# Four chained layers on one Trainium2 core: padded scan sums, layer 3's own image pool, and the next pair's first step made in layer 3

## The chip, the cores and the metric

The kernel runs on one core of a Trainium2 chip. A core has five engines, each with its own instruction queue that is worked off in order: TensorE (PE in the profile, with PEld for its weight loads), VectorE (DVE), ScalarE (ACT), GpSimd (POOL) and SyncE (SP), which here only issues DMAs. The engines share an on-chip memory of 128 partitions; TensorE writes its sums to a second one, PSUM. The metric is the time of one execution on the device in microseconds, as the median of several.

## The reference

The input x is 16 images of 192 channels and 64 x 64 points, in float32. Four layers follow one another, and each adds its result to x. Ahead of each layer x is group-normalised (32 groups of 6 channels).

```
x = x + L0(_gn(x))     # a small network on each point of each channel (tanh, sigmoid)
x = x + L1(_gn(x))     # x and its four shifts by one point, times a 192 x 960 matrix
x = x + L2(_gn(x))     # four state-space scans over the image
x = x + L3(_gn(x))     # depthwise 3x3, 5x5, 1x7, 7x1, then a 192 x 192 matrix, batch norm, clip(0, 6)
```

Layer 2 runs each image through four scans (k = 0 row by row, 1 column by column, 2 and 3 the same backwards) with N = 16 states per channel:

```
dA = jnp.exp(d[..., None] * A)                          # d = delta = softplus(dts + bias)
h = dA * h + (d * u)[..., None] * Bt[:, :, None, :]
y = jnp.einsum('bkdn,bkn->bkd', h, Ct)
...
ys = jnp.moveaxis(ys, 0, -1) + xs * Ds.reshape(K, D)[None, :, :, None]
```

and adds the four results up in image order. Layer 3's batch norm takes its mean and variance over all 16 images, so that its last step can only come at the very end.

## The kernel before

**Tiling.** Two images make a pair: 384 rows of 4096 points, in three tiles (j = 0, 1, 2; NT = 3) of 128 partitions. There are 8 pairs. For each, `front` (L372) does layers 0 and 1 and the projections of layer 2, `scans` (L782) does layer 2, and `layer3` (L1053) does layer 3 up to z, its result ahead of the batch norm. The front of the next pair runs beside the scans of this one: `scans` drives it as a generator, a few instructions per step. Pair 0's front runs alone at the start, and after pair 7 a last stage (L1174 on) computes the batch norm, clips and adds.

**Scans.** For each tile j, direction k (in ORDER = 1, 3, 0, 2) and chunk m of 1024 points there is one entry t of `todo`, 48 per pair, and for each t there are 16 steps, one per state n. Each step s = 16 t + n is a product on DVE (`product`, L910: the spread row of B times du = delta * u), a scan on DVE (`scan`, L913), a copy of the last state on ACT, and a product with C on POOL. Beside them `load_c` fetches the row of C (SP), `decay` makes dA three steps ahead (ACT), and `spread` (L897) brings a row of B into PSUM with two matmuls, two steps ahead. Its PSUM tile is one of two, so it waits for the scan two steps before. `add_up` (L931) sums the products over the states in PSUM on PE, LATE = 4 steps behind, and after the last state ACT copies the sum to X (row-wise directions) or Xt (column-wise).

**The step of a chunk.** delta and du of chunk t + 1 are made during chunk t by `step_rest` (L867): at n = 4 its four matmul instructions write v, ACT applies softplus, and at n = 8 POOL makes du. v and the sum ysum share one PSUM tile: v waits until ACT has copied the sum of the chunk before out (at n = 3), and the next sum's first state (at n = 5) waits until softplus has read v. At n = 4 the loop issues, in this order, the product, the scan, `decay(s + 3)`, `spread(s + 2)`, and then `step_rest`. The load of the rows for chunk t + 2 (`load_dt`, at n = 4, SP) shares one buffer with that of t + 1, so it waits for v.

**The end of a tile.** `finish` (L963) adds Xt to X in four pieces, each followed by two bn_stats for the group norm of layer 3, and stores X to `x3_d`. For tiles 0 and 1 this lies in the next tile's first chunk; for tile 2 (adds on DVE) it comes after the last step.

**Order.** Everything in `scans` is kept in program order on its engine (`_Engines(tc, True)`). Everything in `layer3` is ordered at compile time by a scheduler with program order as its priority. Memory is given out pool by pool, in the order in which the pools are opened; pools that are opened after others were closed lie where those were, and their first use waits for the last use of what lay there.

**Layer 3.** It loads the three tiles of x3 into the middle of a padded tile xp of 70 x 70 points (L1064), zeroes the edges and builds diagonal matrices of the taps' weights on POOL (L1070 to L1077), does the group norm, normalises (L1085), and then goes over four row blocks c and three tiles j. Of the 29 taps of a group (c, j), GP_TAPS = 8 are products on ACT added up by POOL (L1106), PE_TAPS = 7 are matmuls with the diagonals (L1111), which also add POOL's sum g (L1123), and the other 14 are multiply-adds on DVE into the same PSUM tile (L1129; the last one writes y). There are two such PSUM tiles. Then PE multiplies the three y with the 192 x 192 matrix (L1143), ACT copies z out, DVE takes its statistics, and z is stored. The first pieces of the next pair's scans (its load of xn, dt and bp, the normalising, v, delta, du, at L984 to L990) follow after that.

**Last stage.** For each of the 24 tiles z and x3 are loaded, ACT applies scale, shift and relu, DVE clips and adds, and the sum is stored (L1221 to L1231).

Of the kernel before, what the change touches and what calls it, by code (L numbers as in the profile page):

```python
# [22 lines left out]
P = 128  # L23
C = 192
NT = 3
# [24 lines left out]
PE_TAPS = 7  # L50
GP_TAPS = 8

# [52 lines left out]
def conv_preact_kernel(ctx: ExitStack, tc: tile.TileContext, a: dict):  # L105
# [10 lines left out]
    x3_d = dram.tile([npair, NT * P, L], F32, name="x3_d")  # L116
# [3 lines left out]
    wt_d = dram.tile([GR, NG, 2 * P], F32, name="wt_d")  # L120

# [79 lines left out]
    with tc.tile_pool(name="prep", bufs=1) as prep, tc.tile_pool(  # L201
# [83 lines left out]
        for part, w in (  # L285
            (wc[:, :, 2:5, 2:5], w3x3),
            (wc[:, :, 3, :], w1x7),
            (wc[:, :, :, 3], w7x1),
        ):
            nc.vector.tensor_tensor(part, part, w, ALU.add)  # L290

# [18 lines left out]
    sets = [Made(n) for n in range(2)]  # L310

# [25 lines left out]
    def group_norm(E, st, stat, ps, gm, rstd):  # L337

        mv = stat.tile([P, NT, 2], F32, name="mv", tag="mv")
        mean = stat.tile([P, NT], F32, name="mean", tag="mean")  # L340
        d2 = stat.tile([P, NT], F32, name="d2", tag="d2")
        half = stat.tile([P, NT], F32, name="half", tag="half")
        E.dve.memset(half, -0.5)
        for j in range(NT):
            E.dve.bn_aggr(mv[:, j, :], st[:, j, :, :].rearrange("p c s -> p (c s)"))
        E.dve.tensor_copy(mean, mv[:, :, 0])

        def mean_of(src):
            s = ps("gn_sum")
            for jo in range(NT):  # L350
                for n, (b, ji) in enumerate(INTO[jo]):
                    E.pe.matmul(
                        s[:, jo : jo + 1],
                        grp[:, b, :],
                        src[:, ji : ji + 1],
                        start=(n == 0),
                        stop=(n == len(INTO[jo]) - 1),
                    )
                yield
            return s[:, :NT]  # L360

        s = yield from mean_of(mean)
        E.dve.tensor_scalar(gm, s, 1.0 / 6.0, None, ALU.mult)
        E.dve.tensor_tensor(d2, mean, gm, ALU.subtract)
        E.dve.tensor_tensor(d2, d2, d2, ALU.mult)
        E.dve.tensor_tensor(d2, d2, mv[:, :, 1], ALU.add)
        s = yield from mean_of(d2)
        E.dve.tensor_scalar(d2, s, 1.0 / 6.0, 1e-5, ALU.mult, ALU.add)
        E.gps.tensor_tensor(rstd, d2, half, ALU.pow)
# [412 lines left out]
    def scans(i, o, st3, nxt):  # L782

        E = _Engines(tc, True)
        with ExitStack() as es:
# [5 lines left out]
            two = pool("l2two", 2)  # L791
# [8 lines left out]
            X = one.tile([P, L], F32, name="X")  # L800
# [18 lines left out]
            def load_bp(t):  # L819
                if t < T:  # L820
                    j, k, at, first = todo[t]
                    bps[t] = two.tile([BP, LC], BF16, name="bp")
                    E.sp.dma_start(out=bps[t], in_=o.bp[k, :, at : at + LC])

            def load_dt(t):
                if t < T:
                    j, k, at, first = todo[t]
                    dts[t] = one.tile([32 + RD, 512], F32, name="dt")
                    src, r = (o.dtp, RD * (k // 2)) if k % 2 else (o.dt, RD * (2 + k // 2))
                    for h in range(2):  # L830
                        E.sp.dma_start(
                            out=dts[t][32 * h : 32 * h + RD, :],
                            in_=src[r : r + RD, at + 512 * h : at + 512 * h + 512],
                        )

            def load_xn(j):
                if j < NT:
                    xns[j] = one.tile([P, L], F32, name="xn")
                    E.sp.dma_start(out=xns[j], in_=row_tiles(o.x2)[:, j, :])
# [27 lines left out]
            def step_rest(t):  # L867


                j, k, at, first = todo[t]  # L870
                dt = dts.pop(t)
                v = py.tile([P, LC], F32, name="v", tag="ysum")
                for h in range(2):
                    rows = slice(32 * h, 32 * h + RD)
                    E.pe.matmul(
                        v[:, 512 * h : 512 * h + 512],
                        dtw[rows, k, j, :],
                        dt[rows, :],
                        start=True,
                        stop=True,  # L880
                    )
                delta = two.tile([P, LC], F32, name="delta")
                E.table(SOFTPLUS)
                E.act.activation(delta, v, AF.Softplus, bias=dtb[:, k, j : j + 1])
                yield
                du = two.tile([P, LC], F32, name="du")
                E.gps.tensor_tensor(image(du), image(delta), seq(xns[j], k, at, LC), ALU.mult)
                made[t] = delta, du
# [42 lines left out]
            def add_up(s):  # L931
# [8 lines left out]
                to = (Xt if k % 2 else X)[:, at : at + LC]  # L940
                if n == 1:
                    ysum[t] = py.tile([P, LC], F32, name="ysum", tag="ysum")
                    for c in range(LC // 512):
# [5 lines left out]
                        elif k != ORDER[0]:  # L949
                            E.pe.matmul(ysum[t][:, cs], ident, to[:, cs], start=True, stop=False)  # L950
# [9 lines left out]
                if n == N - 1:  # L960
                    E.act.copy(to, ysum[t])

            def finish(j):  # L963

                def add(c):
                    x = X[:, 1024 * c : 1024 * c + 1024]
                    eng = E.gps if j < NT - 1 else E.dve
                    eng.tensor_tensor(
                        image(x), image(x), columns(Xt)[:, 16 * c : 16 * c + 16, :], ALU.add
                    )  # L970

                def stats(c):
                    for h in range(2 * c, 2 * c + 2):
                        E.dve.bn_stats(st3[:, j, h, :], X[:, 512 * h : 512 * h + 512])

                for at in range(10):
                    if at in (0, 2, 4, 6):
                        add(at // 2)
                    if at in (3, 5, 7, 9):
                        E.later(lambda c=at // 2 - 1: stats(c))  # L980
                    yield
                E.sp.dma_start(out=row_tiles(x3_d[i])[:, j, :], in_=X)

            load_xn(0)  # L984
            load_dt(0)
            load_bp(0)
            norm_xn(0)
            for _ in step_rest(0):
                pass
            load_dt(1)  # L990
# [8 lines left out]
            gstep = iter(())  # L999
            for s in range(total):  # L1000
# [4 lines left out]
                if n == 2:  # L1005
                    load_bp(t + 1)
                if n == 4:
                    load_dt(t + 2)
# [4 lines left out]
                scan(s)  # L1013
                if s + 3 < total:
# [9 lines left out]


# [4 lines left out]
                elif n == 4:  # L1030
                    gstep = step_rest(t + 1) if t + 1 < T else iter(())
                    next(gstep, None)
# [18 lines left out]
            E.between()  # L1051

    def layer3(i, st3):  # L1053
        E = _Engines(tc, False)
        with tc.tile_pool(name="l3s", bufs=1) as stat, tc.tile_pool(name="l3x", bufs=1) as xk, tc.tile_pool(
            name="l3w", bufs=1
        ) as w_, tc.tile_pool(name="l3", bufs=2) as wk, tc.tile_pool(
            name="l3_pt", bufs=2, space=PSUM
        ) as pt, tc.tile_pool(name="l3_pz", bufs=4, space=PSUM) as pz:
            S = HW + 6  # L1060
            xp = xk.tile([P, NT, S, S], F32, name="xp")
            inside = slice(3, 3 + HW)
            for j in range(NT):
                nc.sync.dma_start(  # L1064
                    out=xp[:, j, inside, inside], in_=image(row_tiles(x3_d[i])[:, j, :])
                )
            pw = load("pw", [P, len(BLOCKS), P], w_)
            diag = w_.tile([P, NT, PE_TAPS, P], F32, name="diag")
            for edge in (slice(0, 3), slice(3 + HW, S)):
                nc.gpsimd.memset(xp[:, :, edge, :], 0.0)  # L1070
                for j in range(NT):
                    nc.gpsimd.memset(xp[:, j, inside, edge], 0.0)
            for j in range(NT):
                for t, (ty, tx) in enumerate(TAPS[:PE_TAPS]):
                    nc.gpsimd.tensor_scalar(
                        diag[:, j, t, :], ident, wc[:, j, ty, tx : tx + 1], None, ALU.mult
                    )  # L1077
# [5 lines left out]
            for j in range(NT):  # L1083
                v = xp[:, j, inside, inside]
                normalise(nc.vector, v, v, gm, rstd, j)  # L1085
            zst = stat.tile([P, NT, 8, 6], F32, name="zst")
            def window(j, c, rows, tap):
                return xp[:, j, c + tap[0] : c + tap[0] + rows, tap[1] : tap[1] + HW]
# [3 lines left out]

            own = PE_TAPS + GP_TAPS
            for c in range(4):
                ys = []
# [42 lines left out]
                for jo in range(NT):  # L1138
                    z = wk.tile([P, 1024], F32, name="z")
# [18 lines left out]
            nc.sync.dma_start(out=zstat_d[i], in_=zmv.rearrange("p j s -> p (j s)"))  # L1158

    def pair(i, q, more):  # L1160

        with tc.tile_pool(name="st3", bufs=1) as p3:
            st3 = p3.tile([P, NT, 8, 6], F32, name="st3")
            scans(i, sets[q], st3, None if more is None else (more, sets[1 - q]))
            layer3(i, st3)

    with tc.tile_pool(name="f_ps", bufs=1, space=PSUM) as ps:
        for _ in front(0, sets[0], _Engines(tc, False), Banks(ps, 8), True):
            pass
    for i in range(npair):  # L1170
        pair(i, i % 2, i + 1 if i + 1 < npair else None)


    with tc.tile_pool(name="fin", bufs=1) as fin, tc.tile_pool(  # L1174
# [45 lines left out]
        with tc.tile_pool(name="last", bufs=2) as lp:  # L1220
            for i in range(npair):  # L1221
                for j in range(NT):
                    z = lp.tile([P, L], F32, name="zl")
                    r = lp.tile([P, L], F32, name="rl")
                    nc.sync.dma_start(out=z, in_=row_tiles(z_d[i])[:, j, :])
                    nc.scalar.dma_start(out=r, in_=row_tiles(x3_d[i])[:, j, :])
# [3 lines left out]
                    nc.vector.scalar_tensor_tensor(r, z, 6.0, r, ALU.min, ALU.add)  # L1230
                    nc.sync.dma_start(out=row_tiles(out[i])[:, j, :], in_=r)  # L1231
# [107 lines left out]
```

## Time and profile before

| | |
|---|---|
| time, median of 3 runs (28011.66 to 28014.21) | 28012.72 us |
| profiled execution: time, and its span | 28007.89 us, 28006.0 us |
| start to the first scan of pair 0 | 1213.6 us |
| first to last scan of a pair, pairs 0 to 6 / pair 7 | 2954 to 2962 / 2784 us |
| last scan of a pair to first scan of the next | 366 us, 7 times |
| last layer-3 multiply-add of pair 7 to the end | 396.5 us |
| busy: DVE, PE, POOL, ACT | 86%, 83%, 74%, 58% |

A line of the timeline has the start and the duration in us, the engine (a name that ends in q is its queue issuing a DMA), the line of the kernel, the operation, output <- inputs, and how many such instructions were merged. In brackets is the idle time of the engine just before, and what ended it. Line L64 is a helper through which all of `scans` and `front` issues, so there the tiles tell the operations apart. A matmul of float32 is two instructions, so one group's seven diagonals in two halves are 28. A line of the waits names the engine and what it was about to do, what it waited for, the total in us, how often, and the longest.

### The profile page before, as it was taken

To read this page: it belongs to the slowest core of one execution; us is meant where nothing else is said; L and a number is where in the kernel's file an instruction comes from. 1 tells how busy PE (TensorE), PEld (TensorE's weight loads), DVE (VectorE), ACT (ScalarE), POOL (GpSimd) and SP (SyncE) were. 2 spreads that over 40 slices of the span, in tenths; PEclk is the share of its full clock that TensorE was granted. 3 is DMA by queue.
4 is the path that set the end of the run, shared out by engine and by line. 5 is a ranking of instruction groups with operands and counts; after the bars stand their busy time and mean duration, and the time that the engine had idled before them with its cause. 6 is when DMAs were issued, how large, how long until landed. Compare 5 with 4: busy or idle time off the path is not lost. (4 is left out here: it accounts for less than half of the span.)

```text
span 28006.0 us, 208082 instructions
## 1 busy us (share of the span) xinstructions
PE 23305.0 (83%) x57140; PEld 9559.7 (34%) x57140; DVE 24196.3 (86%) x15397; ACT 16122.6 (58%) x23044; POOL 20813.2 (74%) x10440
## 2 busy tenths in 40 slices
PE   8799977999689986999779997899968998676663
PEld 4343323333233332333324332333323333222221
DVE  0399988999899998999989998899989999899994
ACT  7388445774468643785548844577446864344433
POOL 2388877887778876888768887788777887677772
PEclk9899988999899998999889998899989999888886
DMA  4489864898568973898748986589856897367765
GB/s 100 132 222 224 215 201 141 220 220 220 157 181 226 220 220 116 220 224 219 212 124 222 224 215 202 141 221 220 219 155 182 226 219 218 114 189 192 192 183 234
DMA packets 2008001, 5448.00 MB, mean 195 GB/s; under 512 B 550392, under 2 KB 550616, under 8 KB 1989424
## 3 DMA queue, kind: packets, MB, share of 16 engines
q1 hardware_dynamic: 1782192, 4578.95, 56.4%
q0 software_dynamic: 221184, 805.40, 15.2%
q10 hardware_dynamic: 3456, 50.33, 0.4%
q8 instruction: 455, 7.45, 0.1%
q14 instruction: 714, 5.85, 0.1%
HBM read 3896.19 MB, written 329.51 MB: 151 GB/s over the span
## 5 line engine op out<-in xcount | busy, mean ns | idle before, releaser
L64 POOL TENSOR_TENSOR h<-h,cb 128x1024 f32<-128x1024 f32 x6144 | 14856.3, 2464 | 4181.8 <-ACT state L64 3664.7
L64 DVE TENSOR_TENSOR_SCAN h<-dA,state,pbt 128x1024 f32<-128x1024 f32 x4608 | 10809.9, 2346 | 675.9 <-ACT dA L64 91.2
L64 PE MATMUL ysum<-h,ident 128*128 128x512 f32 x18432 | 9464.1, 639 | 208.2 <-DMA h<-h 138.6
L64 DVE TENSOR_TENSOR pbt<-du,pbt 128x1024 f32<-128x1024 f32 x6144 | 7434.8, 1210 | 658.0 <-PE pbt L64 619.6
L64 ACT ACTIVATE dA<-delta,t_alog 128x1024 f32<-128x1024 f32 x6144 | 7036.6, 1146 | 4.9
L64 PEld LDWEIGHTS ysum<-h,ident 128*128 128x128 f32 x18432 | 3777.4, 206 | 4520.3 <-issue 3923.8
L64 ACT COPY state<-h 128x1 f32<-128x1 f32 x6144 | 1145.0, 186 | 6401.7 <-DVE h L64 6324.1
L64 PE MATMUL pbt<-bp,pick 96*128 96x512 bf16 x8192 | 2686.3, 412 | 2127.4 <-DVE h L64 2106.9
L64 DVE TENSOR_TENSOR_SCAN h<-dA,pbt 128x1024 f32<-128x1024 f32 x1536 | 3509.1, 2285 | 228.5 <-DMA h<-h 52.6
L64 PE MATMUL p<-t,wts 96*128 96x512 f32 x5376 | 2707.6, 602 | 136.1 <-ACT t L64 135.9
L64 PE MATMUL p<-m,wms 128*96 128x512 f32 (+1 forms) x5376 | 2653.6, 595 | 0.9 <-ACT lu L64 0.3
L64 ACT ACTIVATE t<-p,bias 96x512 f32<-96x512 f32 x2688 | 1809.2, 679 | 1046.2 <-PE p L64 1027.8
L64 PEld LDWEIGHTS <-pick 96*128 96x128 bf16 x8192 | 711.9, 101 | 4920.9 <-DVE h L64 3256.2
L1106 POOL TENSOR_TENSOR l_g<-l_g,l_m 128x1024 f32<-128x1024 f32 x672 | 1615.1, 2405 | 452.3 <-ACT l_g L1102 346.6
L64 PE MATMUL l_p<-l_xp,w1s 128*128 128x512 f32 x3920 | 1844.7, 599 | 3.4 <-POOL l_xp L64 3.3
L1129 DVE SCALAR_TENSOR_TENSOR l_p<-xp,wc,l_p 128x1024 f32<-128x1024 f32 x1248 | 1589.8, 1287 | 262.6 <-PE l_p L1123 231.7
L64 PE MATMUL pbt<-bp,pick_mix 96*128 96x512 bf16 x4096 | 1282.7, 395 | 559.6 <-DVE h L64 555.3
L64 POOL DMA_DIRECT2D h<-h x1536 | 1359.0, 885 | 494.9 <-POOL h L64 427.9
L1111 PE MATMUL l_p<-xp,diag 128*128 128x512 f32 x2688 | 1289.0, 639 | 332.0 <-DVE l_y L1129 281.3
L64 PEld LDWEIGHTS p<-t,wts 96*128 96x128 f32 x5376 | 1007.9, 190 | 1292.6 <-issue 903.8
L64 ACT ACT_TABLE_LOAD x1111 | 1425.4, 1283 | 19.4
L64 POOL TENSOR_TENSOR du<-delta,xn 128x1024 f32<-128x1024 f32 x384 | 1034.5, 2694 | 452.7 <-ACT delta L64 452.7
(219 smaller groups left out, 17750.1 us busy)
## 6 DMA issues: line engine op xcount, KB each, us to landing
cb<-cp_d SPq DMA_DIRECT2D x2048, 512.0 KB
cb<-c_d SPq DMA_DIRECT2D x2048, 512.0 KB
h<-h POOLq DMA_DIRECT2D x1536, 512.0 KB, 7.1
cb<-cp_d SPq DMA_DIRECT2D x2048, 256.0 KB
cb<-c_d SPq DMA_DIRECT2D x2048, 256.0 KB
m<-l_xn SPq DMA_DIRECT2D x3072, 128.0 KB
bp<-bp_d SPq DMA_DIRECT2D x384, 192.0 KB
f0x<-in_x SPq DMA_DIRECT2D x96, 512.0 KB
```

The lines of the kernel that those rows point to most:

```text
L64: return self._tc.keep_in_program_order(call(*args, **kw))
L1106: nc.gpsimd.tensor_tensor(g, g, m, ALU.add)
L1111: nc.tensor.matmul(ps[:, cs], diag[:, j, t, :], window(j, 16 * c + 8 * h, 8, tap), start=(t == 0), stop=False,)
L1129: nc.vector.scalar_tensor_tensor(image(y if tap is TAPS[-1] else ps), window(j, 16 * c, 16, tap), factor(j, tap), image(ps), ALU.mult, ALU ...
```

## The change

**The sum X stays padded.** X becomes a tile of 70 x 70 points in a pool `over` that lives as long as the kernel; its edges are zeroed once. `add_up`, `finish` and the statistics work on its inside (`rows_of`). `x3_d` holds padded images, so they are stored and loaded as whole rows of a partition. Layer 3 reads tile 2 from X itself; it loads only tiles 0 and 1, and X is stored to `x3_d` in layer 3.

**Layer 3's images have their own pool.** The two loaded tiles stand in the pool opened last (`l3x`), behind a tile of 16 KB that nothing uses (`gap`); the diagonals are now made once, at the start, and loaded from `diag_d`. The group norm of tile 0, which needs tiles 0 and 1 alone, is done during the last chunk of the scans, and tile 0 is normalised by itself, in four pieces, ahead of the rest.

**A tap goes from DVE to PE.** PE_TAPS is 8, so 13 taps remain on DVE.

**The next pair's first step is made in layer 3.** `begin` loads xn, dt and bp, normalises, and makes delta and du ahead of row block c = 2; its v takes one of the two PSUM tiles. The buffers of xn, bp, dt, delta and du move to `over`.

**delta's product ahead of the spread.** At n = 4 the first part of `step_rest` now comes right after the scan, before `decay(s + 3)` and `spread(s + 2)`.

**The last stage** loads padded x3 tiles and stores the result from z's buffer.

```diff
-PE_TAPS = 7
+PE_TAPS = 8
...
+    X = over.tile([P, S, S], F32, name="X")
+    inside = slice(3, 3 + HW)
+    nc.gpsimd.memset(X, 0.0)
...
+    def begin(o, psum):
+        E = _Engines(tc, False)
+        k = ORDER[0]
+        xn = over.tile([P, L], F32, name="xn")
+        nc.sync.dma_start(out=xn, in_=row_tiles(o.x2)[:, 0, :])
+        dt = load_dt(nc.sync, o, k, 0)
+        bp = load_bp(nc.sync, o, k, 0)
+        normalise(nc.vector, xn, xn, o.gm, o.rstd, 0)
+        delta = over.tile([P, LC], F32, name="delta", tag="delta", bufs=2)
+        make_delta(E, psum(), delta, dt, k, 0)
+        du = over.tile([P, LC], F32, name="du", tag="du", bufs=2)
+        nc.gpsimd.tensor_tensor(image(du), image(delta), columns(xn)[:, : LC // HW, :], ALU.mult)
+        return xn, bp, delta, du
...
-            load_xn(0)
-            load_dt(0)
-            load_bp(0)
-            norm_xn(0)
-            for _ in step_rest(0):
-                pass
-            load_dt(1)
+            xns[0], bps[0], *made[0] = begun
+            next_dt(1)
...
+            gm0, rstd0 = (p3.tile([P, NT], F32, name=f"first{n}") for n in range(2))
+            gn0 = group_norm(E, st3, p3, ps, gm0, rstd0, range(2))
...
                 scan(s)
+                if n == 4:
+                    gstep = step_rest(t + 1) if t + 1 < T else iter(())
+                    next(gstep, None)
                 if s + 3 < total:
                     decay(s + 3)
                 if s + 2 < total:
                     spread(s + 2)
...
+                if t == T - 1 and n > 2:
+                    next(gn0, None)
...
-                elif n == 4:
-                    gstep = step_rest(t + 1) if t + 1 < T else iter(())
-                    next(gstep, None)
...
+            gap.tile([P, GAP * 256], F32, name="gap")
+            xps = [xk.tile([P, S, S], F32, name=f"xp{j}") for j in range(NT - 1)] + [X]
+            for j in range(NT - 1):
+                nc.sync.dma_start(out=xps[j], in_=x3_d[i, j])
+            for r in range(0, HW, 16):
+                v = xps[0][:, 3 + r : 19 + r, inside]
+                normalise(nc.vector, v, v, gm0, rstd0, 0)
+            diag = w_.tile([P, NT, PE_TAPS, P], F32, name="diag")
+            nc.sync.dma_start(out=diag, in_=diag_d)
...
+            nc.sync.dma_start(out=x3_d[i, NT - 1], in_=X)
...
+                if c == 2 and o_next is not None:
+                    begun = begin(o_next, lambda: pt.tile([P, 1024], F32, name="l3_p"))
```

## The prediction

> **What bounds the kernel now.** I read the page first (parts 1, 2 and 5), then windows of one pair boundary, its timeline, and the lists of waits of DVE and PE.
>
> ```profile
> span 28006.0 us, 208082 instructions
> PE 23305.0 (83%) x57140; PEld 9559.7 (34%) x57140; DVE 24196.3 (86%) x15397; ACT 16122.6 (58%) x23044; POOL 20813.2 (74%) x10440
> ```
>
> DVE leads. In a pair's scans it alternates a product (1210 ns) and a scan (2346 ns); where no next-pair work runs beside them a step takes 3.57 us, which is DVE alone. In the trace, pairs 0 to 6 need 2954 to 2962 us from first to last scan, pair 7 2784 us. From a pair's last scan to the next pair's first lie 366 us, seven times alike (365.8 to 366.7). I cut these at the first and last of layer 3's multiply-adds: A = 71.3, B = 267.5, C = 27.2 us. Windows of the first boundary (columns after the length: busy us of PE, PEld, DVE, ACT, POOL; clock; DMA share; GB/s):
>
> ```profile
> 4172.00:4244.00 72.00, 33.00 (x79) 15.95 (x78) 20.85 (x26) 15.86 (x15) 39.91 (x40) 0.67 0.50 124
> 4244.00:4512.00 268.00, 214.40 (x501) 86.14 (x501) 229.94 (x190) 107.05 (x103) 179.48 (x76) 0.90 0.05 20
> 4512.00:4538.00 26.00, 9.88 (x16) 3.05 (x14) 6.76 (x8) 8.50 (x10) 2.85 (x1) 0.57 0.49 176
> ```
>
> A and C are latency: no engine is full. In B, DVE (86%) and PE (80%) nearly tie. The timeline shows the chains of A, of one round of B, and of C:
>
> ```profile
> 4170.22 2.35 DVE L64 TENSOR_TENSOR_SCAN h<-dA,state,pbt 128x1024 f32<-128x1024 f32 x1
> ...
> 4180.37 2.33 POOL L64 TENSOR_TENSOR h<-h,cb 128x1024 f32<-128x1024 f32 x1
> 4186.33 1.01 ACT L64 COPY X<-ysum 128x1024 f32<-128x1024 f32 x1 [13.54 <-PE ysum L64]
> 4203.46 20.00 SPq L1064 DMA_DIRECT2D xp<-x_d  x3
> 4216.31 2.41 DVE L319 TENSOR_SCALAR xp<-xp,gm,rstd 128x4096 f32<-128x4096 f32 x1 [3.52 <-DMA xp<-x_d]
> 4218.78 14.73 PE L1111 MATMUL l_p<-xp,diag 128*128 128x512 f32 x28 [6.18 <-DVE xp L319]
> 4243.79 6.59 DVE L1129 SCALAR_TENSOR_TENSOR l_p<-xp,wc,l_p 128x1024 f32<-128x1024 f32 x5 [13.27 <-PE l_p L1123]
> ...
> 4453.78 12.43 PE L1111 MATMUL l_p<-xp,diag 128*128 128x512 f32 x28
> 4466.14 1.93 PE L1123 MATMUL l_p<-l_g,ident 64*64 64x512 f32 x8
> 4491.77 8.85 PE L1143 MATMUL zp<-l_y,t_pw 128*128 128x512 f32 x20
> ...
> 4511.46 6.44 PE L1143 MATMUL zp<-l_y,t_pw 128*128 128x512 f32 x8 [10.84 <-DVE l_y L1129]
> 4530.66 2.41 DVE L64 TENSOR_SCALAR xn<-xn,gm,rstd 128x4096 f32<-128x4096 f32 x1 [11.01 <-DMA xn<-x_d]
> 4537.17 1.23 DVE L64 TENSOR_TENSOR pbt<-du,pbt 128x1024 f32<-128x1024 f32 x1 [4.09 <-POOL du L64]
> ```
>
> A: the last h product sits behind 15 of the 21 diagonals that POOL builds from 4171.65 (8.74 us); then X is summed, stored, read back, normalised, and POOL adds up seven taps before DVE can start. C: after the last z, load, normalise, delta and du come one behind the other. The waits inside the scans:
>
> ```profile
> DVE pbt L64 <- PE pbt L64: 619.6, 635, 7.7
> ...
> PE ysum L64 <- ACT delta L64: 236.1, 193, 4.2
> ```
>
> DVE waits for spreads. Sorted by state number, 305 us of the idle time before products lie at state 8 of a chunk: PE, in order, holds the sum of state 1 until softplus has freed the PSUM tile, and the spread for state 8 queues behind.
>
> **What the Trainium skill says.** "TensorE: Matmul & The Clock Gate", What's actually happening: an idle window of about 3.4 us drops the clock to half. The trace agrees: 0.44 us a matmul instruction in the x20 line, 0.80 in the x8 line after 10.84 us of idling. "DMA: Bandwidth & Descriptors", Specifications: pieces under 512 B miss line rate. It agrees: the padded loads, in rows of 256 B, hold SP 20.0 us for three, and the first lands 12.8 us after issue, where the X store of the same 2 MB lands in 6.3. "SBUF — State Buffer", Who interferes with whom: copies on DVE can be blocked by GpSimd for a whole instruction. Consistent: the mean's [128x3] copy averages 1885 ns inside the scans, 602 outside.
>
> **The change part by part** (first boundary's clock; last scan ends E = 4172.6).
>
> *A, 71.3 to 45.* Without diagonals on POOL the last h product starts at about 4173; PE's sums before it end at 4176.9, so X's adds start 5.8 us earlier (4181.5), the last add ends at 4191.3, the statistics at 4193.6. Tile 0 is stored long before, so its padded load goes out in the last steps (SP issues its last cb at about 4161), into memory that the front has left. Its normalising (2.4 us in four pieces) follows E; eight ACT products (1.16) and seven POOL adds (2.41, 16.9 in all) end at about 4194. The diagonals now come by DMA into l3w, which by the order of the pools lies where Xt was: after the last add, 4191.3, plus 1.57 MB at the X store's rate (6.3 us for 2.1 MB) with some start, 4198. PE then takes 14.73 + 4 x 0.444 = 16.5 for 32 instructions (eight taps) and 1.93 for g: 4216.5, A = 44; I take 45. Tile 1 and 2's constants (10 us from statistics to rstd) and normalising (3.5 each) end near 4211, under PE's cover; uncovered they would cost up to 7. X is not reloaded; its store has the loads' cover. Ends: 24 if the diagonals need not wait, 60 if the loads collide.
>
> *B, 267.5 to 245.* Each of 12 groups loses one DVE tap: 12 x 1.287 = 15.4 us. PE gains 4 instructions a group: 48 x 0.444 = 21.3. Per round of three groups, today: DVE 42 x 1.287 + 6 x 0.69 = 58.2, PE 3 x (12.43 + 1.93) + 28 x 0.443 = 55.5, measured round 65.9. After: DVE 54.3, PE 60.9: PE becomes the bound. Walking today's order with the new durations (two PSUM tiles, diagonals waiting for DVE to free one) gives 62.1 a round, with PE idle only 1 us, so warm. First group to last: 62 + 2 x 62.1 + 53.7 = 240. The next pair's first step adds on DVE 2.41, POOL 2.85 (idle a third of the time, but ahead of later taps' adds), ACT 1.1 plus one or two table loads of 1.28, four loads on SP ahead of the last z stores (their buffers are free since the scans ended; DMA 5% busy), and on PE 1.13 us of v plus a PSUM tile held till softplus ends; there PE has no cover, so 5: 245. Ends: 235 and 272 (no gain).
>
> *C, 27.2 to 10.* The load, normalising, delta and du are gone from here. Left: z (6.4), its copies and statistics to 8.3 us after the last multiply-add, spread beside them, a table load and exp (2.4), scan: 10. Ends 7 and 16. Pair 7 has no C and no begin.
>
> Sum: A 8 x 26 = 208; B 7 x 22.5 + 27.5 = 185; C 7 x 17 = 119: **512 saved**.
>
> *First group norm inside the last chunk.* Its DVE operations at their in-scan means (copy 1.9, add of variance 1.7, the rest 2) and one wait for PE, 6.5 a pair: **+52** (20 to 90).
>
> *Delta's product ahead of the spread*, 376 chunks. Gain: delta no longer stands behind a spread that waits for DVE. In the trace, delta would end 1.9 us sooner on average (v as soon as PE is free and ACT has copied the old sum out, softplus at once); taking the smaller of that and each idle time at state 8 gives 257 us. Loss: v's 1.13 us and the wait for that copy now stand before state 6's spread; laid onto each chunk, the product of state 6 comes 0.3 us later, 112 in all. ACT's exp behind the softplus is needed three steps (10.7 us) later and waits unseen; front work behind it on ACT may wait about 1 us. SP's dt load, ahead of cb loads, is released earlier. Net 145; I take **130 saved** (305 saved to 100 lost).
>
> *Padding elsewhere.* The final stage is DMA-bound (share 1.01, 427 GB/s); 24 tiles grow by 0.41 MB: 9.9 MB / 427 = **+23** (to +60 if storing from z delays its next load). Diagonals and memset at the start lie on POOL, 0.88 us busy from 50 to 100: **+3**.
>
> Total -512 + 52 - 130 + 23 + 3 = -564. The profiled execution took 28007.9 (span 28006.0 plus 1.9), 4.8 under the median 28012.7; so 27,449, **27,450 us**.
>
> **Rivals.** *More overlap*: diagonals come early (A 24: -168) and the scans gain 260 (-130): 27,150. For: DVE then is free from 4194; against: pool order. *PE eats the tap*: B stays at 272 (8 x 27.5): 27,670. For: PE's 60.9 against DVE's 54.3; against: its idle goes. *Slower: v blocks PE.* ACT's copy of the old sum ends 1.0 us after state 4's scan on average, 2.9 in a tenth of chunks; v waits for it with the spread behind, while ACT stops for v. It needs 564 - 130 = 434 us over 376 chunks, 1.15 us net each, to cancel everything; at 1.6 it gives +600 and 28,180. Against: a spread has 3.57 us before DVE misses it. *The head start is void*: the compiled order puts tile 0's work and the next step behind the old chains: A 65, B 270, C 20, scans nothing, additions 78 kept: about 28,000.
>
> **How the numbers follow.** Mine 0.50, more overlap 0.17, PE eats the tap 0.25, v blocks 0.05, void 0.03. Hence faster by over 0.2% (about what a measurement can tell) 0.92, within 0.03, slower 0.05. The range 27,200 to 27,700 leaves out half of the first rival and the last two.
>
> **What would show it.** After: no L1075 diagonals in layer 3; A near 45, B near 245 with PE above 90% and DVE near 83%, C near 10; "PE ysum <- ACT delta" under 60 us; idle at state 8 under 100, at state 6 up to 120; final stage 20 longer. Wrong if B stays above 265, or if a new wait of v on ACT grows past 400.

## The result, and the profile after

| | before | after |
|---|---|---|
| time, median (5 runs each) | 28013.31 us (28011.66 to 28014.65) | 27887.51 us (27875.76 to 27897.42) |
| profiled execution: span | 28006.0 us | 27885.6 us |

The ratio is 0.9955, with an interval of 0.9941 to 0.9968: faster by 0.45%. The forecast was 27,450 us (range 27,200 to 27,700), so 126 of the 564 us came. The first line and the engines of the page of after:

```profile
span 27885.6 us, 208702 instructions
...
PE 23499.7 (84%) x57652; PEld 9648.3 (35%) x57652; DVE 24195.1 (87%) x15397; ACT 16075.9 (58%) x23023; POOL 20709.2 (74%) x10241
```

The span fell by 120 us and DVE's busy time by 1 us, though 96 multiply-adds of 1.29 us are gone from it: those 123 us came back as small operations of the group norms (+73 in the trace), normalising (+38) and adds to X (+17), some of them slower beside POOL, as shown below. The stages of the two traces, cut as in the prediction (S from the first to the last scan of a pair, A from a pair's last scan to the first multiply-add of layer 3, B from the first to the last multiply-add, C from there to the next pair's first scan), means over the pairs in us:

| stage | before | after | all pairs, after less before | forecast |
|---|---|---|---|---|
| start to the first scan | 1213.6 | 1203.3 | -10 | +3 |
| S, pairs 0-6 / pair 7 | 2958.5 / 2784.4 | 2956.0 / 2806.0 | +4 | -78 |
| A | 71.4 | 51.5 | -159 | -208 |
| B, pairs 0-6 / pair 7 | 267.5 / 267.3 | 280.0 / 266.8 | +87 | -185 |
| C | 27.3 | 9.9 | -122 | -119 |
| last multiply-add to the end | 396.5 | 475.8 | +79 | +23 |
| sum | | | -121 | -564 |

The forecast's sum and the measured one differ by 443 us: 272 of them lie in B, 82 in S, 56 after the last multiply-add and 49 in A, while the start and C came out 16 better. The windows of the boundary after pair 1 (length, then busy us of PE, PEld, DVE, ACT, POOL; clock; DMA share; GB/s), with B in the second row:

```profile
7458.00:7510.00 52.00, 29.97 (x83) 15.61 (x82) 26.01 (x26) 19.04 (x18) 35.73 (x14) 0.74 0.25 88
7510.00:7790.00 280.00, 237.34 (x549) 94.87 (x548) 213.05 (x177) 105.58 (x102) 172.95 (x74) 0.91 0.06 25
7790.00:7816.00 26.00, 11.03 (x20) 3.13 (x19) 21.20 (x21) 11.33 (x16) 8.44 (x5) 0.57 0.68 218
```

In B, DVE's share went from 86% to 76% (213.05 of 280) and PE's from 80% to 85%. Neither is full: something else holds both back. The waits of PE name candidates (engine and what it was about to do, what it waited for; total, times, longest):

```profile
PE zp L1196 <- ACT z L1203: 100.8, 32, 4.9
PE v L66 <- ACT Xt L66: 89.6, 78, 3.8
...
PE v L66 <- ACT X L66: 84.7, 78, 1.1
...
PE l_p L1164 <- ACT delta L832: 73.4, 7, 10.7
```

The first (PE wants a PSUM bank for z that ACT has not yet copied out) was smaller before:

```profile
PE zp L1143 <- ACT z L1150: 31.5, 8, 4.1
```

The last is new: seven times, once per begin, PE's diagonals stand for 10.5 us on average behind the next pair's softplus. The two v waits come with the earlier delta in the scans (the first of them was 20.6 us before).

### The profile page after: what moved, and what is told of

It reads as the page before. It is cut to its first block, busy times and chain, and to the rows that moved or that the text cites. A ratio compares the mean times of both kernels' runs of the same rounds, so it can differ in the third digit from the quotient of the medians.

```text
span 27885.6 us, 208702 instructions
## 1 busy us (share of the span) xinstructions
PE 23499.7 (84%) x57652; PEld 9648.3 (35%) x57652; DVE 24195.1 (87%) x15397; ACT 16075.9 (58%) x23023; POOL 20709.2 (74%) x10241
## 5 line engine op out<-in xcount | busy, mean ns | idle before, releaser
L1182 DVE SCALAR_TENSOR_TENSOR l_p<-xp,wc,l_p 128x1024 f32<-128x1024 f32 x768 | 990.4, 1290 | 246.9 <-PE l_p L1176 220.9
L66 PEld LDWEIGHTS p<-m,wms 128*96 128x96 f32 (+1 forms) x5376 | 944.1, 176 | 743.2 <-issue 359.1
L66 ACT ACTIVATE m<-m,bias,sp 96x512 f32<-96x512 f32 x1344 | 1078.0, 803 | 169.6 <-DMA m<-l_xn 164.6
```

Of the source, the lines that this page charges most:

```text
L66: return self._tc.keep_in_program_order(call(*args, **kw))
L1182: nc.vector.scalar_tensor_tensor(image(y if tap is TAPS[-1] else ps), window(j, 16 * c, 16, tap), factor(j, tap), image(ps), ALU.mult, ALU ...
```

## The experiments

My theory after the result: each part works as the diff says, but three of them put PE, or a load, behind ACT's or SP's queue, where a sum of busy times doesn't see it. The rival: PE is simply full (the prediction's "PE eats the tap"). No kernel below leaves out a part of the reference. Unless said otherwise, an edit is made to the changed kernel. Ratios are to the kernel before on the same chip; its median lay between 28,009 and 28,033 us on the chips of these runs, so a difference of some 20 us between two runs is read from their stages. S itself scatters: in the traces of the runs that leave the scans as they are it lies between 2955.4 and 2959.7 us for pairs 0 to 6.

### Parts undone one at a time

**Three z buffers in the last stage.** `zl` gets `bufs=3`.

> The changed kernel, with three instead of two buffers for z in the last stage. Theory (the chain load, ACT, add, store through two z buffers sets the last stage, with the loads waiting on SP for the stores): the time from the last multiply-add to the end goes from 476 to about 420 us, the DMA share there back to 1.0, the whole to about 27,830. Rival (the padded loads and the larger transfers themselves are slower): it stays above 460.

27844.41 us, ratio 0.9932 (0.9917 to 0.9947). The last stage took 407.3 us in place of 475.8; A, B and C moved by less than 1 us (S by 3.7, which is scatter). The timeline of after shows why (SPq and ACTq issue DMAs):

```profile
27648.49 5.25 SPq L1290 DMA_DIRECT2D out<-zl  x2
...
27661.93 11.08 SPq L1282 DMA_DIRECT2D zl<-z_d  x2
27677.59 3.80 ACT L1284 ACTIVATE zl<-zl,shift,scale 128x4096 f32<-128x4096 f32 x1 [28.67 <-DMA zl<-z_d]
```

The result is now stored from z's buffer, so the next z may be loaded only when that store has landed; its load goes out 13 us after the store's issue. ACT then stands for 28.67 us. The windows of the last stage, first after, then with three buffers:

```profile
27700.00:27750.00 50.00, 0.00 (x0) 0.00 (x0) 8.85 (x2) 7.60 (x2) 0.00 (x0) 0.50 0.91 375
```

```profile
27650.00:27700.00 50.00, 0.00 (x0) 0.00 (x0) 13.28 (x3) 11.40 (x3) 0.00 (x0) 0.50 1.01 430
```

The DMA share goes back to 1.01, that of before, and the stage is 11 us longer than before's 396.5, which leaves 11 for the padding.

**No head start** (`gn0` and the four early pieces taken out; tile 0 is normalised with the others).

```diff
-                if t == T - 1 and n > 2:
-                    next(gn0, None)
...
-            for j in range(1, NT):
+            for j in range(NT):
```

> The changed kernel without the head start of tile 0: no group norm in the last chunk, tile 0 normalised with tiles 1 and 2. Theory (the head start costs the scans 15 to 19 us a pair, because its DVE operations and the four pieces are put between the scans and wait for POOL, and gains little, because the diagonals and the second group norm let PE start only 34 us after the last scan): first to last scan of a pair falls by 15 to 19 us, A grows from 51.6 to about 58, sum about -80 us over 8 pairs. Rival (the padded loads slow the last chunk, and the head start is what shortened A): the last chunk stays at 4.5 us a step and A goes back to 66 or more, +110 us.

27868.38 us, ratio 0.9942 (0.9927 to 0.9956). A step of the last chunk is back from 4.53 to 3.60 us, which is 15 us a pair. S falls by 10.9 (18.6 in pair 7). But A grows by 4.2 and B by 6.0, the latter all in PE's wait for z banks (148.7 us in place of 100.8, over 8 pairs): the early work saves about what it costs. The spans differ by 20 us where the theory had 80; the rival's A of 66 did not come either (55.7).

**The begin after layer 3**, in place of ahead of row block 2.

```diff
-                if c == 2 and o_next is not None:
-                    begun = begin(o_next, ...)
...
             nc.sync.dma_start(out=zstat_d[i], ...)
+            if o_next is not None:
+                begun = begin(o_next, ...)
```

> The changed kernel with the next pair's first step made after the last row block of layer 3 instead of ahead of block 2. Theory (the step holds one of two PSUM tiles for 10 us a pair because softplus is late in ACT's order): B goes from 280.0 to 267, C from 9.9 to about 25, so +1 to +3 us a pair. Rival (B is long because of the eighth tap on PE, the step costs little): B stays above 275, +12 us a pair or more.

27805.42 us, ratio 0.992 (0.9905 to 0.9934). B falls from 280.0 to 266.4, and C stays short: 8.3, where the theory had 25. The timeline of after at the begin:

```profile
7633.29 2.08 PE L828 MATMUL l_p<-dt,t_dtw 12*128 12x512 f32 x4
...
7643.16 1.28 ACT L832 ACT_TABLE_LOAD   x1
7644.46 1.11 ACT L832 ACTIVATE delta<-l_p,t_dtb 128x1024 f32<-128x1024 f32 x1
7645.62 7.94 PE L1164 MATMUL l_p<-xp,diag 128*128 128x512 f32 x14 [10.26 <-ACT delta L832]
```

v is done at 7635.4, but ACT comes to its softplus 9 us later: ahead of it in ACT's queue stand products for POOL's sum, each of which waits for a POOL add. All that time v holds one of the two PSUM tiles that the taps need. With the begin after layer 3 the same operations are:

```profile
7755.94 1.13 PE L828 MATMUL l_p<-dt,t_dtw 12*128 12x512 f32 x4
7757.12 1.11 ACT L832 ACTIVATE delta<-l_p,t_dtb 128x1024 f32<-128x1024 f32 x1 [4.33 <-PE l_p L828]
...
7758.31 2.85 POOL L847 TENSOR_TENSOR du<-delta,xn 128x1024 f32<-128x1024 f32 x1 [29.09 <-ACT delta L832]
```

They end at 7761, under the last multiply-adds. So C's gain never needed the place inside the row blocks.

**v in two of the z banks**, the begin left where it is: `make_delta` in two halves of 512, each in a `zp` bank.

> The changed kernel with the next pair's step still ahead of row block 2, but its v in two of the four PSUM banks of z instead of in a tile of the depthwise sums; softplus then comes in two halves. Theory (what costs 13 us a pair is that v holds one of the two tiles of the depthwise sums while softplus waits behind ACT's tap products): B goes from 280.0 to 266 to 271 us, C stays under 10. Rival (the step's own work on DVE, ACT and POOL in the middle of layer 3 is the cost, wherever v stands): B stays at 276 or more.

27792.1 us, ratio 0.9921 (0.9904 to 0.9937), B 267.6. Nearly the same gain, with v, softplus and du of the begin still inside: the loss was the tile held, not this work.

**Seven taps on PE** (`PE_TAPS = 7`, 14 on DVE).

> The changed kernel with seven taps on PE and fourteen on DVE, as before. Theory (moving the tap only swaps which of two nearly equal engines sets the pace): B stays at 280 within 3 us, A falls by 2, the whole within 30 us of the changed kernel. Rival (the eighth tap made PE the bound and costs the 27 us that were expected of B): B falls by 10 us or more, the whole by 80 or more. Second rival (the tap earned its 15 us, and only the next pair's step hides that): B grows by 10 or more.

27872.61 us, ratio 0.9944 (0.9927 to 0.996). B is 279.0 in pairs 0 to 6, as the theory said. In pair 7, which has no begin, it is 262.8 with seven taps and 266.8 with eight. Here the moved tap is no gain at all.

**Delta behind the spread**, as in the kernel before (the block at n = 4 goes back below `spread`).

> The changed kernel with delta's product behind the spread again, as before the change. Theory (the edit earned what was forecast for it, about 130 us, and the last chunk hides it in the sum): first to last scan of pairs 0 to 6 grows by 15 to 22 us, of pair 7 by less than 5, the whole by 110 to 150 us. Rival (the edit only moved idle time from state 8 to state 6): within 30 us of the changed kernel.

28031.67 us, ratio 1.0008 (1.0 to 1.0017). The scans of pairs 0 to 6 take 20.6 us more each, those of pair 7 0.8 less, together 143, and PE's old wait is back:

```profile
PE ysum L66 <- ACT delta L66: 240.2, 197, 4.4
```

It is 60.7 us in after. Without this one part the change gives nothing.

### What the early pieces cost

**The four pieces behind the scans**, by keeping them in DVE's program order (`normalise(_InOrder(tc, nc.vector), ...)`).

> The changed kernel with the four pieces that normalise tile 0 kept in program order on DVE, so that they come behind the last scan and tile 2's statistics instead of between the last scans; the early group norm stays in the last chunk. Theory (the pieces cost the last chunk 8 to 10 us, and A does not need them that early, because PE starts the diagonals only 34 us after the last scan, late by the second group norm, which POOL's adds slow down): the last chunk falls from 4.53 to about 3.95 us a step, A stays within 50 and 53, sum -70 to -100 us. Rival (the early start of tile 0 is what shortened A): A grows by as much as the scans lose, or more, and the sum is zero.

27887.16 us, ratio 0.9955 (0.994 to 0.997). A last-chunk step takes 4.05 us; the scans give 8.5 us a pair and B takes 6.6, so the forecast 70 to 100 us did not come. A stayed at 52.2, which speaks against the rival; what the theory left out is B, where PE's wait for z banks rose from 100.8 to 161.4 us. The timeline of after shows what a piece costs between scans:

```profile
7424.67 0.82 DVE L341 TENSOR_SCALAR xp<-xp,first,first 128x1024 f32<-128x1024 f32 x1 [1.33 <-POOL first L66]
...
7428.04 2.35 POOL L66 TENSOR_TENSOR h<-h,cb 128x1024 f32<-128x1024 f32 x1 [3.41 <-ACT state L66]
7428.77 2.17 DVE L341 TENSOR_SCALAR xp<-xp,first,first 128x1024 f32<-128x1024 f32 x1
```

The first piece takes 0.82 us with POOL idle; the second takes 2.17 beside POOL's product, and ends 0.55 us after it. "SBUF — State Buffer" of the Trainium skill, Who interferes with whom, says that a DVE `tensor_scalar` can enter a mode in which it shares ports with GpSimd, and that the one issued second is then fully blocked for the other's whole instruction. This agrees.

**Begin after, three z buffers and seven taps together.**

> Three z buffers in the last stage, the next pair's step after the last row block, and seven taps on PE, all at once in the changed kernel. Theory (the three losses lie in different stages and add up): last stage 407, B 262 to 264, A 50.5, C 8 to 9, the whole 27,885 - 68 - 95 - 40 = about 27,680. Rival (the seven taps let DVE set the pace again once the step is gone, as in the kernel before): B stays at 267 and the whole near 27,720.

27688.0 us, ratio 0.9885 (0.987 to 0.99): as expected.

**The same, and the pieces behind the scans.**

> The three edits together (three z buffers in the last stage, the begin after layer 3, seven taps) and, besides, the four normalising pieces of tile 0 kept behind the scans on VectorE. Theory: what the scans gain (8 us a pair, last chunk 4.54 to about 4.05 a step) comes back in B, since the pieces then stand between the scans and the layer: S -8 a pair, B +6 to +8 (264.6 to about 271), time 27,690 within 20 us of the three edits alone. Rival: without the eighth tap and the begin inside the layer the first multiply-adds no longer stand behind the pieces, so B stays near 265 and the time falls by 60, to about 27,630.

27694.91 us, ratio 0.9879 (0.9864 to 0.9894). B goes from 264.6 to 269.9, a last-chunk step from 4.54 to 4.04: a trade, as the theory said, though S fell by only 2.4 (7.8 in pair 7), which for pairs 0 to 6 is within its scatter.

**The same three, and the pieces on ACT.**

```diff
-                normalise(nc.vector, v, v, gm0, rstd0, 0)
+                nc.scalar.activation(v, v, AF.Identity,
+                    bias=less0[:, 0:1], scale=rstd0[:, 0:1])
```

> The three edits together and, besides, tile 0's four normalising pieces made on ScalarE (scale and offset by one activation each) in place of VectorE. Theory: the pieces cost what they cost because VectorE is what the scans wait for and holds them 2.2 us each, and ScalarE has room there: last chunk 4.54 to about 4.05 us a step, S 7 to 8 us a pair less, A and B as with the three edits alone (50 and 265), time about 27,625. Rival: ScalarE's copies of the state and its decays are then late by as much, or the start of the layer waits for them: time within 15 us of 27,690.

27645.9 us, ratio 0.9863 (0.9846 to 0.9879); on the same chip the version before this one took 27694.91. The last-chunk step is 4.05 us, A (49.8) and B (264.9) stay, S falls by 5.5 (11.1 in pair 7). ACT takes the pieces at 1.25 us each, and nobody waits for them:

```profile
7410.05 1.25 ACT L1130 ACTIVATE xp<-xp,less,first 128x1024 f32<-128x1024 f32 x1
```

### Why the eighth tap gained nothing

By then B was 265 in its best form, and 240 was forecast for eight taps without the begin. The timeline of after, from the z of row block 0 on:

```profile
7509.59 14.15 PE L1164 MATMUL l_p<-xp,diag 128*128 128x512 f32 x32
...
7545.85 7.13 PE L1196 MATMUL zp<-l_y,t_pw 128*128 128x512 f32 x16
...
7553.85 1.17 ACT L1155 ACTIVATE l_m<-xp,wc 128x1024 f32<-128x1024 f32 x1 [1.28 <-POOL l_g L1159]
...
7555.98 0.56 ACT L1203 COPY z<-zp 128x512 f32<-128x512 f32 x1
...
7556.60 2.01 PE L1196 MATMUL zp<-l_y,t_pw 128*128 128x512 f32 x2 [3.62 <-ACT z L1203]
...
7560.97 1.17 ACT L1155 ACTIVATE l_m<-xp,wc 128x1024 f32<-128x1024 f32 x1 [1.28 <-POOL l_g L1159]
7562.04 0.56 ACT L1203 COPY z<-zp 128x512 f32<-128x512 f32 x1
...
7562.66 2.07 PE L1196 MATMUL zp<-l_y,t_pw 128*128 128x512 f32 x2 [4.05 <-ACT z L1203]
...
7564.52 11.78 PE L1164 MATMUL l_p<-xp,diag 128*128 128x512 f32 x24
...
7585.00 14.15 PE L1164 MATMUL l_p<-xp,diag 128*128 128x512 f32 x32
...
7585.12 17.23 DVE L1182 SCALAR_TENSOR_TENSOR l_p<-xp,wc,l_p 128x1024 f32<-128x1024 f32 x13 [4.03 <-PE l_p L1176]
```

ACT's copies of z stand in its queue among the products l_m, and each l_m waits for a POOL add. So PE gets its z banks back at POOL's pace and stands for 3.62 and 4.05 us. The diagonals of the next group stand behind z in PE's queue, and DVE pays with 4.03 us. From the first group of 32 diagonals to the same group of the next row block (7509.59 to 7585.00) this round takes 75.4 us; the last such round, which has only one wait for a z bank, takes 68.5. Two kernels take this apart, both with the begin after layer 3 and eight taps (27805.42 us and B 266.4 without a further edit).

**GpSimd's taps from 8 to 7** (`GP_TAPS = 7`, so 14 on DVE again).

> The begin after layer 3, eight taps on TensorE, and GpSimd's taps cut from 8 to 7, so that VectorE keeps the 14 of the kernel before. It tells what keeps a round with eight taps at 68 us. If TensorE's own order does it (its idle ahead of z and behind y, and the half-clock matmuls after it), a shorter sum on GpSimd changes little and VectorE's added tap (1.29 us a group) adds to it: B from 266.4 to between 268 and 280, time 27,820 to 27,900. If the products on ScalarE and their sum on GpSimd do it (ScalarE's z copies stand behind products that wait for GpSimd's adds), the round falls towards VectorE's 58.2 and TensorE's 60.9: B 250 to 258, time 27,680 to 27,740.

27746.99 us, ratio 0.99 (0.9883 to 0.9916), B 263.4: between the two expectations, so no verdict by the sum. The waits say more: PE's wait for z is gone from the list, and its wait for DVE's y has risen from 85.4 to 161.6 us. One limit went and another, DVE with 14 taps, came.

**z copied by DVE in place of ACT.**

```diff
-                        nc.scalar.copy(z[:, 512 * h : 512 * h + 512], ps)
+                        nc.vector.tensor_copy(z[:, 512 * h : 512 * h + 512], ps)
```

> The begin after layer 3, eight taps on TensorE, and z copied out of PSUM by VectorE in place of ScalarE. Theory: in a round TensorE waits some 2.2 us for a bank that ScalarE's z copy frees late (112 us in all), and runs half-clock matmuls after it (1.6 us); with both gone B falls by up to 4 x 3.8 = 15 from 266.4, less what VectorE's copies (6 of some 0.7 us a round) put ahead of its taps: B 255 to 262, time 27,720 to 27,775. Rival: the copies stand on VectorE where TensorE waits for y, so the loss moves there: B 266 to 280, time 27,805 to 27,910.

27622.18 us, ratio 0.9856 (0.9842 to 0.9871). B is 244.7 us, below the range of either expectation. The same stretch of its timeline, from row block 0:

```profile
7480.83 14.15 PE L1162 MATMUL l_p<-xp,diag 128*128 128x512 f32 x32
...
7515.42 8.85 PE L1194 MATMUL zp<-l_y,t_pw 128*128 128x512 f32 x20
...
7518.06 0.68 DVE L1201 COPY z<-zp 128x512 f32<-128x512 f32 x1
...
7524.11 12.31 PE L1162 MATMUL l_p<-xp,diag 128*128 128x512 f32 x28
...
7543.38 14.15 PE L1162 MATMUL l_p<-xp,diag 128*128 128x512 f32 x32
```

PE goes from z to the diagonals without a stop. The round (7480.83 to 7543.38) takes 62.55 us and the next two 64.2 and 62.55, where the prediction's walk had 62.1. The six copies add 4.1 us a round to DVE, which has room for them. PE's account in B closes: its waits for z banks (14.3 us a pair without the edit) are gone, and its busy time falls from 233.0 to 224.7, together 22.6, where B fell by 21.7. The theory had sized the second part at 6: matmuls behind a stop are slower (two took 2.01 us above, and the granted clock was 0.52 there), and with the stops such stretches went.

**The same with seven taps.**

> Begin after layer 3, z copied by VectorE, and seven taps on TensorE (14 on VectorE) instead of eight. It asks whether the moved tap is worth anything once TensorE no longer waits for z copies. With eight taps B is 244.7 us a pair. If the tap's price was right all along and was hidden by that wait, VectorE with 42 taps, 6 copies and 6 statistics a round (42 x 1.287 + 12 x 0.69 = 62.3) is the bound and B rises by about 10 to between 252 and 262: time 27,680 to 27,760. Rival: the tap is worth nothing on TensorE in any order, and all of the gain comes from the copies: B 241 to 248, time 27,590 to 27,640.

27754.36 us, ratio 0.9899 (0.9885 to 0.9912), B 262.4. Now the tap is worth 17.7 us a pair, 132 us in all. In the changed kernel with 14 taps on DVE and the begin after layer 3, B is 262 to 265 in all three runs (264.6, 263.4, 262.4).

**The kernel before, with z copied by DVE.**

> The kernel before, with z copied by VectorE as its only edit. It asks whether the wait that ate the tap was there before the change. Theory: hardly; the kernel before waits 31.5 us in all for z's copies, and VectorE (58.2 us of a 65.9 us round) takes 6 x 0.69 = 4.1 us more a round, so B stays between 262 and 275, time within 60 of the kernel before. Rival: the z copies on ScalarE cost the kernel before as much as the changed one: B about 245 to 252, time 27,830 to 27,890.

28069.81 us, ratio 1.0015 (1.0008 to 1.0021), B 271.1 in place of 267.5. In the kernel before the same edit is a small loss: PE hardly waited for the copies there (31.5 us), and DVE's busy time in B grows from 230.2 to 239.6 us. That DVE's 14 taps alone are the reason is not shown: in the changed kernel with 14 taps the same edit loses nothing (B 264.6 to 262.4).

**All that gained, together**: three z buffers, begin after layer 3, z on DVE, pieces on ACT, eight taps.

> What the runs so far point to, together, with eight taps: three z buffers in the last stage (-68), the begin after layer 3, z copied by VectorE, and tile 0's pieces on ScalarE (-45). From 27,622 for the begin after layer 3 with z on VectorE: 27,622 - 68 - 45 = 27,510, within 25, if the gains add up. Rival: the pieces on ScalarE delay its products for the first row block, which the faster rounds no longer hide: B +5 a pair, 27,550.

27512.29 us, ratio 0.9814 (0.98 to 0.9827): the gains add up (27,510 expected), and it beats both kernels.

## Why the prediction was wrong, by its own steps

**A, "71.3 to 45": direction right, 51.5.** The diagonals did come when it said, soon after the last add, but they were not next on PE:

```profile
7477.26 0.32 SPq L1125 DMA_DIRECT2D diag<-diag_d  x1
...
7481.93 3.12 PE L379 MATMUL gn_sum<-mean,t_grp 128*128 128x1 f32 x14 [17.71 <-DVE mean L372]
...
7486.86 2.19 DVE L393 TENSOR_TENSOR d<-d,mv 128x3 f32<-128x3 f32 x1
...
7489.10 3.14 PE L379 MATMUL gn_sum<-d,t_grp 128*128 128x1 f32 x14 [4.06 <-DVE d L393]
7492.11 8.31 PE L1164 MATMUL l_p<-xp,diag 128*128 128x512 f32 x15
```

The diagonals landed at 7484.6 in the trace, 26 us after the last scan's end, as forecast; their matmuls started at 7492.11, behind the second group norm's sums, which the compiled order puts first. The prediction let that norm run "under PE's cover"; it ran in front of the diagonals. The price it gave for that case, "up to 7", on its 44 makes 51, about what came. The norm is slower too (mean at 7480.29 to rstd at 7493.4: 13 us, 9 before); POOL's adds now run beside its small DVE operations, and one of them took 2.19 us for three columns. No run takes this part of A alone, so it is read from the timeline. A saved 19.9 us a pair where 26 were forecast, which is 49 of the 443.

**B, "267.5 to 245": the step that failed.** The sentence is "Walking today's order with the new durations ... gives 62.1 a round, with PE idle only 1 us, so warm". The walk was right on PE and DVE, as the rounds of 62.55 to 64.2 us show once z is copied by DVE. What it left out is ACT's queue: it took a z bank as free when ACT could have copied it, not when ACT got there behind products paced by POOL. With the begin after layer 3 PE stands idle 25 us a pair in B, some 6 a round in place of 1: 14.3 us a pair for z banks and 10.7 for y. The profile of before had the row (31.5 us), and I took it for small. Why it was small then is not shown: with seven taps and the begin after layer 3 it is still 67.7, with eight 112.1. Without the begin, B came to 266.8 for a forecast 240. The begin, "there PE has no cover, so 5", took 13.4 for the same reason: it named the "PSUM tile held till softplus ends" and priced the softplus, not the queue ahead of it. The rival "PE eats the tap" came near in size (272) and is wrong in cause: PE was 85% busy, not full, and with the same taps and z on DVE B is 244.7.

**C, "27.2 to 10": right** (9.9), but not owed to the place that the change chose.

**Group norm in the last chunk, +52: mis-sized.** With the pieces that came to stand there, the last chunk became 15 us longer a pair, 120 in all. About half is the norm itself, the 6.5 a pair of the forecast; the rest are the four pieces. The prediction wrote "Its normalising (2.4 us in four pieces) follows E", but the compiled order put it between the scans, and beside POOL a piece takes 2.17 us, not 0.6. On ACT that half goes.

**Delta ahead of the spread, -130: right.** Undone it costs 143. The sum is better than its two terms: the prediction had 257 gained at state 8 and 112 lost at state 6, and against the run with delta behind the spread the idle time there is 170 less and 60 more; both came out near 60% of their size, which is luck. PE's wait for delta fell from 236.1 to 60.7 us where "under 60" was said, and DVE's wait for spreads from 619.6 to:

```profile
DVE pbt L66 <- PE pbt L66: 458.8, 481, 5.2
```

The two v waits (174 us together) stay far from the 400 that would have meant the slower rival. In the traces, the idle time before the product of state 8 fell from 292 us in all (the prediction read 305) to 129, not "under 100", and at state 6 it rose from 16 to 75, as "up to 120" allowed.

**Scans as a whole.** -20.6 for delta (+0.8 in pair 7) and +15 for the last chunk leave 3 us a pair of pairs 0 to 6, and 6 of pair 7. The 3 us lie in the second-last chunk, which takes 61.1 us in place of 57.6 on average over pairs 0 to 6:

```profile
7376.60 3.77 DVE L341 TENSOR_SCALAR xn<-xn,gm,rstd 128x4096 f32<-128x4096 f32 x1
```

This is the begin's normalising of the next pair's xn. In the source it stands ahead of row block 2, but the compiled order put it, and its load, between the scans of this pair: at the same step of the same chunk in all seven pairs, and also in the kernels whose source has the begin after layer 3. The prediction had priced it as 2.41 us of DVE inside B. Of pair 7's 6 us, 4.4 are one wait of a scan, in the first chunk of its third tile, for the DMA that adds one product to the next; why it waits there stays open.

**Last stage, +23: the wrong end taken.** "To +60 if storing from z delays its next load" stood in the text; it does, and the stage grew by 79: 68 for the wait, which is more than the whole end allowed, and 11 for the padding, which the sum had at 23.

**Start, +3: not foreseen, -10.** xn of the first pair no longer lies in memory that the front has to leave: its load went out at 1031.4 us in place of 1197.1. This is read from the traces alone.

## What to carry to other kernels

When work moves from the engine that is full to one that has room, walk every queue that the new bound waits on, also those of engines that are half idle: ACT was 38% busy in B and still decided the round, because its instructions stood in order behind others that waited for POOL. A wait of 31.5 us in the old profile is no bound on what it becomes: with the eighth tap it was 112.1. An edit that sets a step in one place of the source does not set it in the compiled order: the begin's normalising came to stand between the scans. And a PSUM tile is priced by how long it is held, from the write to the moment the reader's queue gets to it, not by the time that the reader needs.

## What the runs showed of the hardware

A stretch at half clock does not need a pause of 3.4 us here, and is not certain after a shorter one. "TensorE: Matmul & The Clock Gate" of the Trainium skill, What's actually happening, names an idle window of about 3.4 us ahead of the half-rate state. In the kernel with z copied by DVE, the same 32 diagonals behind the same 2.67 us of idling took 14.12 us in row block 0 and 15.79 in row block 1:

```profile
7499.51 14.12 PE L1162 MATMUL l_p<-X,diag 128*128 128x512 f32 x32 [2.67 <-DVE l_y L1180]
```

```profile
7562.06 15.79 PE L1162 MATMUL l_p<-X,diag 128*128 128x512 f32 x32 [2.67 <-DVE l_y L1180]
```

Of the 32 groups behind such a pause in this trace, 16 took 14.1 us and 16 took 15.8. In the slower one shown, six matmuls between 7563.0 and 7566.4 us ran at a granted clock of 0.51, some of them 0.85 us apart in place of 0.43. So a recorded pause shorter than the page's window was followed by half clock in half of the cases; what decides is not shown. Without idling directly ahead of them, 32 groups of 40 took 14.1.

A DVE add of two SBUF operands takes 1.89 us for 128 x 1024 points in the last `finish` while POOL is idle, and 2.88 while POOL adds up its taps beside it. "SBUF — State Buffer", Who interferes with whom, says that a DVE instruction with two SBUF inputs contends with a GpSimd instruction that reads SBUF; this agrees. Two of the four adds are met so in the changed kernel, since POOL's tap sums now start before X is complete. That delays X by 2 us; whether A is shorter without it is not shown.
